# A transformer block in one kernel: the last tiles' norm, logits and hits ahead of other work, square roots moved, the first maxima alone

## The chip, the cores and the metric

The kernel runs on one core of one Trainium2 chip. The metric is the time on the device of one execution, in microseconds; the kernel is run several times and the median is given. A profile is one further execution, recorded by the hardware profiler; its span runs from the first to the last instruction.

Engines by their names in the profile: PE is TensorE (PEld its weight loads), DVE is VectorE, ACT is ScalarE, POOL is GpSimd, and SP, the sync engine, issues most of the DMAs.

## What is computed

A transformer block on x of 8 x 256 x 512 in float32: x = x + attention(layernorm(x)), then x = x + ffn(layernorm(x)). The reference, cut to its core:

```python
qkv = h @ w_qkv                       # 32 query heads, 8 key/value heads, D = 128
scores = einsum('bqhgd,bkhd->bhgqk', q, k) * D ** -0.5
bias = -slopes * sqrt(max(pos_q - pos_k, 0)); -inf where pos_k > pos_q
out = einsum('bhgqk,bkhd->bqhgd', softmax(scores + bias), v) @ w_o

dots = softmax(x @ centroids.T / 0.1)           # 64 clusters
hits = dots > 0.01
query_sel, cluster_sel = any(hits, axis=1), any(hits, axis=0)
row_sel = cluster_sel[assignments]              # one flag for each of 512 columns
dense = x @ weight.T + bias
out = where(query_sel[:, None] & row_sel[None, :], dense, 0)
```

`cluster_sel` asks whether any token of the whole batch hits a cluster, so no output column is settled before the last tile's hits are known.

## The kernel before

The 2048 tokens are 16 tiles of 128 rows (`NT`); four tiles, that is two batch entries, form a pair (`PT_TOK`, `NPAIR` = 4). A unit `u` is one batch entry and one key/value head with its four query heads, so there are 64 units (`NU`), 16 to a pair (`slot` is the unit's place in its pair). One loop runs over the units, and two more passes drain it. Its body is an order written out by hand (`manual_schedule`): each engine executes its instructions in the order in which the program text issues them.

A pass of the loop does in turn the scores of unit u, the softmax of unit u-1, and the value product and output projection of unit u-2:

- `scores(u, 0..2)` (L358) makes keys-by-queries scores in PSUM on PE; DVE scales them and adds the position bias into `s` (L372, L378).
- `over_keys` (L384) takes maxima or sums over the keys on DVE (L387, L388, L390). `over_quadrants` (L392) transposes the result on PE (L397, `tp_r`), finishes it on DVE (L401, L404), writes the row to memory (L406) and reads it back to all partitions (L415), both on SP's queue. Normally one transpose serves the maxima of u and the sums of u-1; a unit for which `alone` holds sends its maxima earlier (`rows_max`). `subtract_max` takes the maxima away, one part on POOL (L422), one on DVE (L425), and ACT takes the exponential (L724, in the last unit L775).
- `attend` (L429) makes the value products (L446, L447) and DVE multiplies by the inverse sums (L450).
- All projections use a seven-product scheme of 2 x 2 blocks. `a_sums` and `b_sums` (L107, L120) make the block sums S1 to S4 and T1 to T4 on POOL (`gp`) or DVE (`ve`). `strassen` (L136) runs step i of a q, k or v projection; `project_out` (L454), called as `w(i)`, that of the output projection. Products 1, 6, 7 and 4 gather in one PSUM bank, and a copy on ACT (L158; L483 into `snap`) must be done before the next of them may be added.
- In some slots a pair of tiles is normalised: `norm_stats` on DVE (L259, L260), `norm_root` on ACT (L267; square root and exponential need different tables, and the load stands as its own instruction), `norm_scale` on DVE (L272, L274), `norm_write` on ACT (L281), and later `transpose_into` on PE (L290) with a copy out of PSUM (L291).
- The feed-forward part of finished pairs goes tile by tile in parts `f(0)` to `f(3)`: `ffn_transpose`, `ffn_logits` with `ffn_exp` and `ffn_dense` (L535), `ffn_bias_add` (L542), and `ffn_hits`, `ffn_qsel`, `ffn_end` (L547 to L562).

In the normal unit the order around the change is:

```python
f(2), norm(0), e(4), e(3), x(0), w(1), x(1), sum_old(), w(5, 6), qq(3), w(2)
rows(), behind_rows(), w(7, 3), norm(2), w(4)
```

where `norm(0)` is statistics and root, `norm(1)`, inside `behind_rows`, the scale and `norm(2)` the write; `e(i)` and `qq(i)` are steps of a k or v and of a q projection.

After the loop come the last four tiles, 12 to 15 (`last` = 12), whose x is complete only then: norms, transposes, logits, exponentials, hits, dense products. Then the row selection: `cnt` counts the hits of each cluster (L862), `csel` is its flag (L864), and `rsel` (L866) spreads it over the 512 columns with the one-hot matrix of the assignments, which `onehot_of_columns` (L580) made in unit 4. At last the output of 16 tiles: three (`SPLIT`) on POOL with a copy `rsel_sb` of the selection (L880 to L882), thirteen on DVE with a predicated copy (L896), stored from the queues of SP and ACT in turn (L897). x and y of the first two pairs were put aside in memory and are read back in unit 63 (L834, four loads of 1 MB).

## Time and profile before

| what | value |
|---|---|
| median of three runs | 1461.13 us (1459.53 to 1461.52) |
| the profiled execution, its own time | 1461.43 us |
| its span | 1459.6 us |
| PE busy | 1412.7 us, 97% of the span |
| DVE busy | 934.0 us, 64% |
| POOL busy | 879.4 us, 60% |
| ACT busy | 369.2 us, 25% |
| granted PE clock, mean | 0.994 of full speed |
| moved by DMA | 189.94 MB, 130 GB/s on average |

In timeline rows the columns are start, length, engine, line, operation, and the tile written, then those read; in brackets stands how long the engine had been idle and what released it. In the rows of stretches each engine has its busy microseconds and its count of instructions, then follow the granted PE clock, the busy share of the DMA engines and GB/s. "SPq" is a DMA issue on SP's queue. Matmuls overlap in the records, so that the length of a row of several is a little more than the time that they take from the engine.

### The profile page before, as it was taken

To read this page: it belongs to the slowest core of one execution; us is meant where nothing else is said; L and a number is where in the kernel's file an instruction comes from. 1 tells how busy PE (TensorE), PEld (TensorE's weight loads), DVE (VectorE), ACT (ScalarE), POOL (GpSimd) and SP (SyncE) were. 2 spreads that over 40 slices of the span, in tenths; PEclk is the share of its full clock that TensorE was granted. 3 is DMA by queue.
4 is the path that set the end of the run, shared out by engine and by line. 5 is a ranking of instruction groups with operands and counts; after the bars stand their busy time and mean duration, and the time that the engine had idled before them with its cause. 6 is when DMAs were issued, how large, how long until landed. Compare 5 with 4: busy or idle time off the path is not lost.

```text
span 1459.6 us, 16530 instructions
## 1 busy us (share of the span) xinstructions
PE 1412.7 (97%) x5859; PEld 1076.0 (74%) x5859; DVE 934.0 (64%) x1708; ACT 369.2 (25%) x648; POOL 879.4 (60%) x885
## 2 busy tenths in 40 slices
PE   8899999999999999999999999999999999999985
PEld 7676777767877678777777677777777777877562
DVE  4467656676566666658655666566756676566766
ACT  3221222421232222331213312142222222122331
POOL 6376867667465654557655466556756675566544
PEclk9999999999999999999999999999999999999998
DMA  5235333443242544424342524424332343243343
GB/s 187 75 132 174 130 95 139 158 145 117 101 159 73 173 140 150 158 83 143 108 147 99 161 86 173 165 110 145 130 114 97 123 174 131 87 159 102 102 145 115
DMA packets 85968, 189.94 MB, mean 130 GB/s; under 512 B 10592, under 2 KB 18784, under 8 KB 85888
## 3 DMA queue, kind: packets, MB, share of 16 engines
q1 hardware_dynamic: 84736, 186.41, 37.2%
q10 hardware_dynamic: 864, 1.57, 0.3%
q8 instruction: 47, 0.77, 0.2%
q0 software_dynamic: 288, 0.92, 0.2%
q14 instruction: 33, 0.27, 0.1%
HBM read 175.77 MB, written 13.11 MB: 129 GB/s over the span
## 4 chain that ended last, share of the span: by engine, by line
PE 86%; DVE 8%; issue 2%; POOL 2%; ACT 1%; DMA 0%; POOLq 0%; DVEq 0%; ACTq 0%
PE ps_oa L468 14%; PE ps_qa L145 13%; PE sc L370 7%; PE ps_oc L468 7%; PE ps_qc L145 7%; PE av L446 6%; PE sc L376 4%; PE ps_ob L468 4%; PE ps_va L145 4%; PE ps_ka L145 4%; PE ps_f L535 4%; PE av L447 3%; PE ps_qb L145 3%; PE ps_vc L145 2%; PE ps_kc L145 2%
## 5 line engine op out<-in xcount | busy, mean ns | idle before, releaser
L500 POOL TENSOR_TENSOR x<-x,snap 128x256 f32<-128x256 f32 x189 | 136.1, 735 | 182.7 <-DVE x L488 110.7
L422 POOL TENSOR_TENSOR s<-s,bc 128x1024 f32<-128x1024 f32 x64 | 151.6, 2368 | 151.7 <-DMA bc<-row_hbm 144.1
L112 POOL TENSOR_TENSOR o_s<-oT 128x256 f32<-128x256 f32 x64 | 47.6, 744 | 191.3 <-DVE oT L450 187.4
L387 DVE TRANSPOSE_TENSOR_REDUCE r<-s 128x32 f32<-128x1024 f32 x128 | 157.9, 1234 | 4.4 <-ACT s L724 4.4
L158 ACT COPY qT<-ps_qa 128x512 f32<-128x512 f32 x128 | 74.7, 583 | 284.5 <-PE ps_qa L145 284.5
L483 ACT COPY snap<-ps_oa 128x256 f32<-128x256 f32 x189 | 70.3, 372 | 278.7 <-PE ps_oa L468 278.7
L468 PE MATMUL ps_oa<-wo,oT 128*128 128x256 f32 x512 | 133.5, 383 | 6.6 <-DVE oT L450 4.2
L724 ACT ACTIVATE s<-s 128x1536 f32<-128x1536 f32 x63 | 93.5, 1484 | 153.1 <-DVE s L425 147.2
L446 PE MATMUL av<-s,v 128*128 128x512 f32 x256 | 131.6, 596 | 0.0
L145 PE MATMUL ps_qa<-xT,wq 128*128 128x256 f32 x512 | 121.1, 380 | 0.8 <-ACT qT L158 0.8
L370 PE MATMUL sc<-qT,kT 128*128 128x512 f32 x256 | 120.3, 592 | 0.0
L145 PEld LDWEIGHTS ps_qa<-xT,wq 128*128 128x128 f32 x512 | 97.1, 190 | 27.6 <-issue 16.0
L468 PEld LDWEIGHTS ps_oa<-wo,oT 128*128 128x128 f32 x512 | 90.6, 190 | 28.6 <-DVE oT L450 8.3
L372 DVE SCALAR_TENSOR_TENSOR s<-sc,alibi 128x512 f32<-128x512 f32 x128 | 88.1, 691 | 29.0 <-PE sc L370 28.1
L378 DVE SCALAR_TENSOR_TENSOR s<-sc,alibi 128x512 f32<-128x512 f32 x64 | 44.3, 692 | 83.7 <-PE sc L376 83.7
L447 PEld LDWEIGHTS av<-s,v 128*128 128x128 f32 x256 | 49.0, 191 | 61.7 <-issue 61.7
L450 DVE TENSOR_TENSOR oT<-av,bc 128x512 f32<-128x512 f32 x128 | 84.1, 683 | 14.2 <-PE av L447 12.3
L388 DVE TRANSPOSE_TENSOR_REDUCE r<-s 128x16 f32<-128x512 f32 x128 | 85.7, 669 | 0.0
L488 DVE TENSOR_TENSOR x<-x,ps_ob 128x256 f32<-128x256 f32 x64 | 27.0, 421 | 79.5 <-PE ps_ob L468 79.4
L447 PE MATMUL av<-s,v 128*128 128x256 f32 x256 | 76.4, 380 | 0.0
L390 DVE TENSOR_TENSOR r<-r 128x16 f32<-128x16 f32 x128 | 72.4, 566 | 4.4
L370 PEld LDWEIGHTS sc<-qT,kT 128*128 128x128 f32 x256 | 48.5, 190 | 33.9 <-issue 29.9
(177 smaller groups left out, 2973.0 us busy)
## 6 DMA issues: line engine op xcount, KB each, us to landing
bc<-row_hbm SPq DMA_DIRECT2D x128, 512.0 KB, 4.9
wq<-in_w_qkv SPq DMA_DIRECT2D x32, 1024.0 KB, 7.7
wo<-in_w_o SPq DMA_DIRECT2D x32, 1024.0 KB, 7.8
alibi<-al_hbm SPq DMA_DIRECT2D x24, 512.0 KB, 8.5
wk<-in_w_qkv SPq DMA_DIRECT2D x16, 512.0 KB, 9.4
wv<-in_w_qkv SPq DMA_DIRECT2D x8, 1024.0 KB, 10.9
x<-in_x SPq DMA_DIRECT2D x16, 256.0 KB, 9.4
al_hbm<-alibi SPq DMA_DIRECT2D x8, 512.0 KB, 9.1
```

The costliest lines, as they stand in the source:

```text
L145: nc.tensor.matmul(bank[:, cols], lhsT=lhsT, rhs=rhs, start=first and j == 0, stop=j == len(mms) - 1, skip_group_check=True)
L370: nc.tensor.matmul(sc, lhsT=kT[:, t0 : t0 + P], rhs=qT[:, hh : hh + 2, t0 : t0 + S], start=True, stop=True)
L372: nc.vector.scalar_tensor_tensor(s[:, hh * S : (hh + 2) * S], sc, D ** -0.5, bias[:, hh : hh + 2, :].rearrange("p h q -> p (h q)"), ALU.mu ...
L387: nc.vector.tensor_reduce(first, s[:, :K0].rearrange("p (j q) -> p j q", q=32), AX.X, op, apply_transpose=True)
L388: nc.vector.tensor_reduce(second, s[:, K0:].rearrange("p (j q) -> p j q", q=32), AX.X, op, apply_transpose=True)
L422: gp(k0, k0, mx, sub)
L446: nc.tensor.matmul(av, lhsT=v[:, i0, vc], rhs=pT[:, hh * S : (hh + 2) * S], start=True, stop=False)
L447: nc.tensor.matmul(av3[:, :, P:S], lhsT=v[:, i0 + 1, vc], rhs=pT[:, K0 + hh * P : K0 + (hh + 2) * P].rearrange("p (h q) -> p h q", h=2), s ...
L450: ve(oT[:, e].rearrange("p k m q -> p k (m q)"), av3, inv[:, hh : hh + 2, :], ALU.mult)
L468: nc.tensor.matmul(bank[:, :HH], lhsT=x[:, e, :], rhs=y[:, e, :], start=first and e == 0, stop=e == 1, skip_group_check=True)
L500: gp(c, c, s, ALU.add)
L724: nc.scalar.activation(s_sb[u - 1], s_sb[u - 1], AF.Exp)
```

## The change

- The norm has four parts now: statistics, root, scale, write. The root goes from behind `f(2)` to behind `w(5, 6)`.
- `onehot_of_columns` goes from ahead of unit 4 to behind its `qq(2)`.
- Unit 0 sends its maxima alone, as the last two units do, and S3 and S4 of the first v weights are made before the loop.
- In the opening, the second pair of tiles gets its scale and write after tile 1 is transposed and copied, and tile 3 is transposed ahead of `k(2)`.
- In pass 64 the value products go ahead of a feed-forward transpose. In pass 65 the hits of tile 11 go ahead of the projection, and tile 13's transpose, tile 14's norm and both logits products of tiles 12 and 13 go into the pass.
- After the loop, maxima, exponentials and hits of the four last tiles go ahead of most dense products; tile 13's product is split in two around the row selection (`ffn_dense` takes `chunks`); the ends of tiles 11 to 13 go ahead of the predicated copies; two products of bias and flag go from POOL to ACT.

```diff
--- before.py
+++ after.py
@@ -509,32 +509,42 @@
     ffn_sb = {}
     SPLIT = (1, 2, 3)
 
-    def ffn_logits(t):
+    def ffn_logits_product(t):
         xnT = xnT_sb[t]
         lg = p_sc.tile([P, 512], F32, tag="sc", name="lg")
         for c in range(NC_H):
             nc.tensor.matmul(lg[:, :NCL], lhsT=xnT[:, c, :], rhs=cent[:, c, :],
                              start=c == 0, stop=c == NC_H - 1)
+        ffn_sb[t] = lg
+
+    def ffn_max(t):
+        lg = ffn_sb[t]
         nmax = small.tile([P, 1], F32, tag="cmax", name="cmax")
         nc.vector.tensor_reduce(nmax, lg[:, :NCL], AX.X, ALU.max, negate=True)
         nc.vector.tensor_scalar(nmax, nmax, 1.0 / TEMPERATURE, None, ALU.mult)
         ffn_sb[t] = lg, nmax
 
-    def ffn_exp(t):
+    def ffn_logits(t):
+        ffn_logits_product(t)
+        ffn_max(t)
+
+    def ffn_exp(t, e=None):
 
         lg, nmax = ffn_sb[t]
-        e = small.tile([P, NCL], F32, tag="e", name="e", bufs=3)
+        if e is None:
+            e = small.tile([P, NCL], F32, tag="e", name="e", bufs=3)
         esum = small.tile([P, 1], F32, tag="esum", name="esum")
         nc.scalar.activation(e, lg[:, :NCL], AF.Exp, bias=nmax, scale=1.0 / TEMPERATURE, accum_out=esum)
         ffn_sb[t] = e, esum
 
-    def ffn_dense(t, w_ffn):
+    def ffn_dense(t, w_ffn, chunks=range(NC_H)):
         xnT = xnT_sb[t]
-        ps = p_acc.tile([P, 512], F32, tag="acc", name="ps_f")
-        for c in range(NC_H):
+        if 0 in chunks:
+            y_sb[t] = p_acc.tile([P, 512], F32, tag="acc", name="ps_f")
+        ps = y_sb[t]
+        for c in chunks:
             nc.tensor.matmul(ps, lhsT=xnT[:, c, :], rhs=w_ffn[:, c, :],
                              start=c == 0, stop=c == NC_H - 1)
-        y_sb[t] = ps
 
     def ffn_bias_add(t, y=None):
         if y is None:
@@ -602,8 +612,9 @@
     found23 = norm_stats(2, 3)
     norm_tile(0, 0)
     sum_x(0, "")
-    normalise(found23, tags=("y", "y"))
+    found23 = norm_root(found23)
     norm_tile(0, 1, tp=tp1, copy=nc.vector.tensor_copy)
+    norm_write(norm_scale(found23), tags=("y", "y"))
     alibi_bias(0)
     sum_weights(gp, wk, (0, 0), D, "S1")
     load_wv(0, 0, wk[0, 0]["S1"])
@@ -616,13 +627,13 @@
     k, q = project_k(0, 0), project_q(0)
     k(1)
     norm_tile(0, 2, tp=tp2, copy=nc.vector.tensor_copy)
+    norm_tile(0, 3)
     k(2)
-    norm_tile(0, 3)
     sum_x(0, "T1 T2 T3 T4")
     a_sums(gp, wq[0], "S3 S4")
-    q(1), q(2), k(6), k(7), k(5), k(4), k(3), q(6), q(7), q(5)
-    sum_weights(ve, wv, (0, 0), HH, "S1 S2")
-    q(4), q(3)
+    q(1), q(2), k(6), k(7), k(5), k(4), k(3)
+    sum_weights(ve, wv, (0, 0), HH)
+    q(6), q(7), q(5), q(4), q(3)
     a_sums(gp, wq[1], "S1 S2 S3")
     w_ffn = None
     y_late = None
@@ -705,14 +716,14 @@
         def norm(part):
             nonlocal found
             if t_norm is not None:
-                found = (lambda _: norm_root(norm_stats(t_norm, t_norm + 1)), norm_scale, norm_write)[part](found)
+                found = (lambda _: norm_stats(t_norm, t_norm + 1), norm_root, norm_scale, norm_write)[part](found)
 
         def max_and_old():
             scores(u, 2)
             over_keys(s_sb[u], r, 0, ALU.max)
             if old:
                 subtract_max(u - 1, 1)
-            if own and slot in (0, 8):
+            if u > 0 and slot in (0, 8):
                 a_sums(ve, wv[p, slot // 8], "S3 S4")
 
         def more_sums():
@@ -727,19 +738,20 @@
             if old:
                 over_keys(s_sb[u - 1], r, 1, ALU.add)
 
-        alone = NU - 2 <= u < NU
+        alone = u == 0 or NU - 2 <= u < NU
 
         def rows_max():
             if alone:
                 over_quadrants(u, r, True, False)
 
         def rows():
-            over_quadrants(u, r, own and not alone, old)
+            if old:
+                over_quadrants(u, r, own and not alone, True)
 
         def behind_rows():
 
             f(3)
-            norm(1)
+            norm(2)
             if own and (slot == 7 or slot == 15 and more_p):
                 sum_weights(ve, wv, (p, 1) if slot == 7 else (p + 1, 0), HH, "S1 S2")
             if more_p and slot == 13:
@@ -755,38 +767,39 @@
             if more_p and slot in (11, 12):
                 norm_tile(p + 1, 2 * (slot - 11) + i)
 
-        if u == 4:
-            onehot_of_columns(asg)
         if bb == 0 and own:
             qq(1), e(1), max_and_old(), e(2), f(0), av(0), e(6), exp_old(), av(1), more_sums(), rows_max(), f(1), e(7), qq(2)
-            f(2), norm(0), e(5), e(4), qq(6), e(3), x(0), w(1), x(1), sum_old(), w(5, 6), qq(7), w(2)
-            rows() if old else over_quadrants(u, r, True, False)
-            behind_rows(), w(7, 3), norm(2), w(4)
+            if u == 4:
+                onehot_of_columns(asg)
+            f(2), norm(0), e(5), e(4), qq(6), e(3), x(0), w(1), x(1), sum_old(), w(5, 6), norm(1), qq(7), w(2)
+            rows(), behind_rows(), w(7, 3), norm(3), w(4)
         elif u < NU - 1:
             e(1), qq(4), e(2), max_and_old(), f(0), e(6), av(0), exp_old(), e(7), av(1), f(1), e(5), qq(5)
-            f(2), norm(0), e(4), e(3), x(0), w(1), x(1), sum_old(), w(5, 6), qq(3), w(2)
-            rows(), behind_rows(), w(7, 3), norm(2), w(4)
+            f(2), norm(0), e(4), e(3), x(0), w(1), x(1), sum_old(), w(5, 6), norm(1), qq(3), w(2)
+            rows(), behind_rows(), w(7, 3), norm(3), w(4)
         elif own:
 
             max_and_old(), f(0), av(0), exp_old(), av(1), rows_max(), f(1)
-            f(2), norm(0), w(1), sum_old(), w(5, 6, 2)
+            f(2), norm(0), w(1), sum_old(), w(5, 6), norm(1), w(2)
             rows(), subtract_max(u, 0), subtract_max(u, 1)
-            f(3), norm(1), w(7)
+            f(3), norm(2), w(7)
             nc.scalar.activation(s_sb[u], s_sb[u], AF.Exp)
-            w(3), norm(2), w(4)
+            w(3), norm(3), w(4)
         elif bb == 0:
-            sum_old(), f(0), av(0), av(1), rows(), f(1), w(1, 5), f(2), w(6, 2, 7, 3, 4), f(3)
+            sum_old(), av(0), av(1), f(0), rows(), f(1), w(1, 5), f(2), w(6, 2, 7, 3, 4), f(3)
         else:
             av(0), f(0), av(1), f(1)
             normalise(norm_stats(last, last + 1), tags=("y", "y"))
+            ffn_hits(t_ffn), ffn_qsel(t_ffn)
             w(1), f(2), w(2, 5, 6)
             ffn_transpose(last)
             w(3)
             found = norm_root(norm_stats(last + 2))
+            ffn_transpose(last + 1, "snap")
             w(7)
-            ffn_logits(last)
+            norm_write(norm_scale(found))
+            ffn_logits_product(last), ffn_logits_product(last + 1)
             w(4)
-            f(3)
 
 
         for dst, src in stores:
@@ -838,24 +851,18 @@
 
 
     y_of = lambda i: y_last[i // 2][:, i % 2, :]
-    norm_write(norm_scale(found))
     ffn_dense(last, w_ffn)
-    ffn_transpose(last + 1, "snap")
     normalise(norm_stats(last + 3))
-    ffn_exp(last)
-    ffn_logits(last + 1)
-    ffn_exp(last + 1)
+    ffn_max(last), ffn_exp(last)
+    ffn_max(last + 1), ffn_exp(last + 1)
     ffn_transpose(last + 2, copy=nc.vector.tensor_copy)
-    ffn_dense(last + 1, w_ffn)
     ffn_transpose(last + 3, "o_s", tp=p_acc.tile([P, 512], F32, tag="acc", name="tpx_late"), copy=nc.vector.tensor_copy)
-    ffn_hits(last), ffn_qsel(last), ffn_bias_add(last, y_of(0))
-    ffn_logits(last + 2)
-    ffn_exp(last + 2)
-    ffn_logits(last + 3)
-    ffn_hits(last + 1)
-    ffn_exp(last + 3)
-    ffn_hits(last + 2), ffn_hits(last + 3)
-    ffn_dense(last + 2, w_ffn)
+    ffn_logits_product(last + 2), ffn_logits_product(last + 3)
+    ffn_max(last + 2), ffn_exp(last + 2)
+    ffn_max(last + 3), ffn_exp(last + 3, work.tile([P, NCL], F32, tag="kT", name="e_last", bufs=2))
+    ffn_dense(last + 1, w_ffn, (0, 1))
+    for i in range(4):
+        ffn_hits(last + i)
 
 
     cnt = p_tp.tile([P, 512], F32, tag="tp", name="cnt")
@@ -864,17 +871,19 @@
     nc.vector.tensor_scalar(csel, cnt[:NCL, :P], 0.0, None, ALU.is_gt)
     rsel = p_tp.tile([P, 512], F32, tag="tp", name="rsel")
     nc.tensor.matmul(rsel, lhsT=csel, rhs=onehot, start=True, stop=True)
-    ffn_dense(last + 3, w_ffn)
-    for i in (2, 3, 1):
+    ffn_dense(last + 1, w_ffn, (2, 3))
+    for i in (2, 3, 0):
         ffn_qsel(last + i)
-    ffn_bias_add(last + 1, y_of(1))
+
+    for i in (2, 3):
+        nc.scalar.activation(y_of(i), bias_bc, AF.Copy, scale=ffn_sb[last + i])
+        gp(y_of(i), y_of(i), x2[last + i], ALU.add)
+    ffn_end(last - 1), ffn_bias_add(last, y_of(0)), ffn_end(last), ffn_qsel(last + 1)
+    ffn_dense(last + 2, w_ffn)
     rsel_sb = work.tile([P, H], F32, tag="s", name="rsel_sb", bufs=3)
     nc.scalar.copy(rsel_sb, rsel)
-
-    for i in (2, 3):
-        gp_y = y_of(i)
-        nc.gpsimd.tensor_scalar(gp_y, bias_bc, ffn_sb[last + i], None, ALU.mult)
-        gp(gp_y, gp_y, x2[last + i], ALU.add)
+    ffn_dense(last + 3, w_ffn)
+    ffn_bias_add(last + 1, y_of(1)), ffn_end(last + 1)
     for t in SPLIT:
         xt, yt = back[0][0][:, t, :], back[0][1][:, t, :]
         gp(yt, yt, rsel_sb, ALU.mult)
@@ -887,8 +896,6 @@
         p, i = divmod(t, TPP)
         if t >= last + 2:
             nc.vector.scalar_tensor_tensor(y_of(i), y_sb[t], ffn_sb[t], y_of(i), ALU.mult, ALU.add)
-        elif t >= last:
-            ffn_end(t)
         if p < NPAIR - 2:
             xt, yt = back[p][0][:, i, :], back[p][1][:, i, :]
         else:
```

## The prediction, made before the changed kernel was run

> **What bounds the kernel now.** I read the page first: how much of the span TensorE is busy, and what the chain that ended last is made of.
>
> ```profile
> span 1459.6 us, 16530 instructions
> PE 1412.7 (97%) x5859; PEld 1076.0 (74%) x5859; DVE 934.0 (64%) x1708; ACT 369.2 (25%) x648; POOL 879.4 (60%) x885
> PE 86%; DVE 8%; issue 2%; POOL 2%; ACT 1%; DMA 0%; POOLq 0%; DVEq 0%; ACTq 0%
> ```
>
> TensorE (PE) is the bound in the loop. The change takes no matmul away, so it can only win in the 46.9 us in which PE is idle (1459.6 - 1412.7). The view of what PE waited for (total, times, longest) says where these lie ahead of the last stretch:
>
> ```profile
> PE ps_oa L468 <- ACT snap L483: 6.1, 10, 1.3
> PE ps_oa L468 <- DVE oT L450: 4.2, 3, 1.6
> PE tpx L290 <- ACT xn L281: 3.6, 1, 3.6
> ...
> PE ps_oa L468 <- ACT kT L158: 2.5, 3, 0.8
> PE ps_va L145 <- DVE wv L116: 2.0, 2, 1.7
> ```
>
> Each has a place in the timeline. A copy of a product out of PSUM is late where ScalarE's queue holds a square root: its table load, then a wait for VectorE's statistics, stand in front of the copy.
>
> ```profile
> 244.53 1.28 ACT L267 ACT_TABLE_LOAD   x1
> ...
> 246.38 0.30 ACT L267 ACTIVATE rstd<-mv,eps 128x2 f32<-128x2 f32 x1 [0.57 <-DVE mv L260]
> ...
> 247.56 1.10 PE L468 MATMUL ps_oa<-wo_t,o_s 128*128 128x256 f32 x4 [0.36 <-ACT snap L483]
> ```
>
> Of the last 18 us PE takes 2.5. The chain in order of time (start, length, what) shows who does the rest:
>
> ```profile
> 1435.48 3.49 PE ps_f L535 x8
> ...
> 1439.70 1.14 PE rsel L866 x2
> ...
> 1445.66 1.29 POOL back_xT L880
> ...
> 1455.99 0.60 POOLq L918
> ```
>
> The dense product stands ahead of the row selection `rsel`; then GpSimd (POOL) writes three tiles while VectorE (DVE) writes thirteen, ending at 1454.62.
>
> **The square roots.** By the instruction order, twelve roots (L267) go behind the copies of out-projection steps 1 and 6, past both snap copies and a q, k or xT copy; the count of table loads does not change. The waits they cause, from the timeline: 0.36, 0.82, 0.18, 0.78, 1.28, 0.82, 0.17, 0.78, 0.17, 0.82 in the loop, 0.89 at 1347 and 1.35 at 1385: 8.4 us, which is the 6.1 and 2.5 of the view less 0.16 at 81 us that no root causes. The new place must hide 1.28 + 0.30 = 1.58 us. At the first one the snap copy of step 6 ends at 249.1, so the root ends at 250.6; the next q copy is due at 250.4 (its bank is wanted in the next unit, 5 us on) and the next snap copy at 252.3. At 273 the slack to the snap is 1.6 us. Cover that goes costs at most 1.58 each. The page "ScalarE: Activation LUTs" of the Trainium skill, section "What ACT_TABLE_LOAD costs", speaks against it: it counts a drain too, about 2.66 us a switch. The trace has none: the load at 1413.26 takes 1.28 and the root starts at 1414.56. With 2.96 for both the root would end at 252.0, still ahead of 252.3, so my sum stands by either; only the 273 kind (three places) would lose about 1.4 each, 4 us in all. Behind a waiting root stand snap 7 and the xn writes; statistics were done 2 to 3 us before. The 1.35 is not won: there DVE ends r (L390) at 1386.63, and PE's tp_r waits for it. That leaves 7.1; I take **6.4**, as some early arrivals will meet a DVE or POOL wait (L450, L112). Bounds 3 and 7.1.
>
> **The one-hot rows.** Six DVE operations stood in front of the third score evacuation of unit 4, one of them 2.46 us beside POOL's L422; PE then waited 1.59 for L450 and 0.17 for o_s. They move behind L450 and the q addition; POOL's iota moves behind the four o_s sums. There DVE waits for the iota until about 122.5 and the key sums end about 125.3, where PE's tp_r comes at about 125.9. **1.6**, bounds 1.0 and 1.8.
>
> **The opening.** (a) The copy of tile 1 goes ahead of reciprocal and shift: the first k product starts at about 9.0 instead of 9.64, but tiles 2 and 3 come 0.4 later and their transposes stand in front of k(2); T1 starts 0.5 earlier. Net 0.3. (b) The S3, S4 sums of wv leave DVE's queue in unit 0, where PE waited 1.7 for them, for 21.5 to about 26.3, when DVE is idle (5.8 us before 27.35) and wv has landed (15.5). In their place tp_r waits for the maxima, which end 0.1 us before L116 did: tp_r at 38.4 and L145 at 38.5 instead of 39.30. Gain 0.8 with (a). (c) The maxima of unit 0 go to memory at about 39 instead of 48.76; on SP's queue the row, its broadcast and behind them wq, alibi and wk all go 9 us earlier. L422 runs at 46, POOL's weight sums at 50 to 59 instead of 59 to 68. So they now lie beside DVE's L390 and L425 in unit 1, and such pairs exclude each other: L425 took 0.68 alone and 1.70 beside POOL. The exponential would start 0.4 earlier, not 0.8, and PE's 1.48 wait for r shrink by 0.6 (L390 there 0.82, free 0.18). Sum **1.2**, bounds -0.5 and 2.8.
>
> **The end.** Four steps.
> In unit 64 the two av products (2.6 us) go ahead of the transpose that waited 3.60 for xn. That wait also halved the clock:
>
> ```profile
> 1393.00:1394.00 1.00, 0.68 (x3) 0.68 (x4) 1.00 (x2) 0.98 (x2) 1.00 (x3) 0.50 0.78 262
> ```
>
> (column PEclk 0.50). PE's tp_r then waits for r (1395.06), so logits start at 1395.3 instead of 1398.12: 2.8 earlier. But the next L450 waits for a broadcast whose row sits behind the 4 MB loads in SP's queue:
>
> ```profile
> SPq L415 <- DMA row_hbm<-row: 6.3, 1, 6.3
> ```
>
> It lands near 1410.1, whatever PE does, against L450 at 1410.79. From there: L450 to 1411.5, maximum 1411.9, statistics 1413.4, exponential and table load 1413.8, root, scale 1414.6, the moved hits 0.87, L481 at 1415.5 (it was 1416.74). Then, each at its trace duration: w(6) about 1416, transposes of tiles 12 and 13, logits of both 1419.7 to 1421.5, w(4), dense(12) 1422.4 to 1425.8, transposes of 14 and 15, exponentials of 12 and 13 behind one 1.28 table load to 1427.4 (both score banks are held until then), logits of 14 and 15 to 1428.9, two exponentials to 1429.9, four hits of 0.63 from 1429.4 to 1431.9, cnt, csel, rsel to **1433.9**. Before it was 1440.8.
> Behind it: DVE does three qsel (0.45), three ends of the L562 kind and two bias additions: alone 0.75 and 0.68 each, 1.7 beside POOL as at 1447.04. Between 3.6 and 5.5 us; I take 4.4, so the thirteen copies start at 1437.5 instead of 1441.48. They take 13 x 0.67 + 2 x 0.74 = 10.2, as no L562 stands between them any more, so DVE ends about 1447.8. ScalarE takes POOL's two bias products (0.8 each, from the xn row) ahead of rsel_sb, which is ready at 1435.1; POOL's additions then end at 1436.3 and its three tiles (10.9) at 1447.2 instead of 1456.6. dense(13) to (15) end at 1442.5, ahead of their readers.
> The stores may bind: 16 tiles are 4.19 MB.
>
> ```profile
> 1444.00:1446.00 2.00, 0.46 (x2) 0.00 (x0) 2.00 (x5) 0.00 (x0) 1.92 (x3) 1.00 1.03 381
> ```
>
> The last column is GB/s: the DMA engines are already full while DVE alone stores a tile each 0.64 us. At 381 GB/s the stores need 11.0 us; the first copy ends about 1438.2, so the last lands about 1450.6 (1.4 us to the first data), against 1450.2 from DVE's end and a landing of 2.4. The page "DMA: Bandwidth & Descriptors", section "Where 436 GB/s comes from", lets HBM bind at about 358 GB/s per core: 11.7 us, an end 0.7 later. The trace shows more on the same stores, so I keep 381. Last landing to the end of the span took 1.2 (1456.0 + 2.4 against 1459.6). New end 1451.8 with nothing else changed: **7.8** won, bounds 4.5 and 9.2 (the lower if hits, transposes or exponentials each wait once more, the higher if DVE's additions run alone).
>
> **Sum.** 6.4 + 1.6 + 1.2 + 7.8 = 17.0. The profiled execution took 1461.43 (1.8 more than its span), so 1444.4; the median of the runs, 1461.13, is 0.3 below that execution, so **1444.1**.
>
> **Rivals.**
> (A) The end is held. If the row's landing keeps L450 at 1410.8, the one chain from there to rsel stretches by a wait or two (DVE's hits stand in front of L481, on which w(6) waits; two score banks serve four tiles), and stores and POOL's additions collide, the end wins 4 instead of 7.8 and the roots 5: 1449.3. For it: handovers between four engines in 25 us. Against: the PE work between is unchanged and each duration is in the trace.
> (B) The opening loses. POOL's sums, 9 us earlier, block L390 and L425 twice, the v copy behind the exponential is 1.5 us later than before instead of 0.4 earlier, and PE's longer idle halves its clock once more, as it did between 62 and 65 us after only 2.2 us (a window at 0.50 cost about 1.7). Opening -2.5 instead of 1.2: 1447.8. For it: L425's 1.70. Against: POOL is done by 59. The same place can go the other way: a shorter wait that does not halve the clock gives 1.7 more, 1442.4.
> (C) Slower: the roots in their new place are late. If the root ends after product 7 wants the copy, each of twelve places pays the 1.58 and, when PE idles over 2 us, a half-clock window of 1.7, 3.3 in all: 39.6 against the 10.6 of the other parts gives 1490; with 1.58 alone, 19.0, it is 1469.5, which I take. It decides from 0.9 us a place. For it: at 273 the slack is 1.6 us, and a root that waits for statistics has waited 4.82 (at 820). Against: those statistics end at 820.6 and the step-6 copy at 823.3.
>
> **How the numbers follow.** My forecast 0.62; (A) 0.17; (B) 0.14; (C) 0.07. Executions before lay within 2 us, so 0.2% (2.9 us) is about what a measurement can tell from no change. The forecast, A and B are all over that; of C's 0.07 I leave 0.02 to a small loss that ends within it: faster 0.93, same 0.02, slower 0.05. Range: the low bounds of all parts together give 1453.1, the high ones 1440.2 and with the clock window 1438.5. I take 1438.5 to 1452.5, which holds the forecast, most of A and B, and not C.
>
> **What would show it.** In the changed profile: PE's waits on snap and kT (L483, L158) behind roots gone but for 0.2 and one at unit 63; at each root the table load stands after a snap copy and PE shows no gap; no 1.59 on L450 near 121 us; the tp_r wait of unit 0 about 1.1 where L116 had 1.7; no half clock at the transpose of unit 64; L450 of unit 65 starting on the broadcast; rsel's end about 41 us after unit 63's exponential ends (1440.8 - 1392.6 = 48 before); POOL's three tiles starting about 15.5 us before the end; DMA rows at 380 GB/s through the last 12 us. I am wrong if rsel moves by less than 4 us against unit 63's exponential, if waits of over 1 us stand at the new roots, or if the stores end later than DVE's last copy plus 4 us.

## The result and the profile after

The changed kernel took 1441.32 us, the median of four runs (1439.02 to 1441.55), beside 1460.33 us of the kernel before: ratio 0.9868 with a 95% interval of 0.9851 to 0.9885, so 19.3 us faster (16.8 to 21.8). In a second comparison (below) the ratio was 0.9891 (0.9875 to 0.9907). The forecast was 1444.1 us; the 17.0 us of its sum lie between the two ratios' 15.9 and 19.3 us. The profiled execution took 1441.13 us, its span 1439.4. Its page, with the chain that ended last:

```profile
span 1439.4 us, 16533 instructions
PE 1407.5 (98%) x5859; PEld 1072.9 (75%) x5859; DVE 928.2 (64%) x1708; ACT 372.2 (26%) x650; POOL 878.2 (61%) x883
PE 90%; DVE 6%; issue 1%; ACT 1%; POOL 1%; DMA 1%; DVEq 0%; POOLq 0%; ACTq 0%; SPq 0%
```

PE executes the same 5859 products, is idle for 31.9 us where it was 46.9, and carries 90% of the last chain where it carried 86%. Its busy time fell too, by 5.2 us. What PE waited for (total, times, longest):

```profile
PE tp_r L397 <- DVE r L390: 5.6, 5, 1.4
PE ps_oa L468 <- DVE oT L450: 2.6, 2, 1.5
...
PE tpx L290 <- ACT xn L281: 2.1, 3, 1.0
...
PE cnt L869 <- DVE hits_any L559: 1.3, 1, 1.3
...
PE ps_oa L468 <- ACT snap L483: 0.4, 1, 0.4
```

The 8.6 us in front of copies out of PSUM (6.1 on snap, 2.5 on kT) are gone but for 0.4 at 78 us, where no root stands; of the wait for oT the 1.59 of unit 4 went too. The 3.6 for xn in unit 64 became 1.0; two shorter waits for xn (0.9 and 0.2) now stand in the opening. The place of a root, in the timeline (the one shown of before at 244 to 248 us):

```profile
243.16 0.37 ACT L483 COPY snap<-ps_oa 128x256 f32<-128x256 f32 x1 [1.30 <-PE ps_oa L468]
243.55 1.28 ACT L267 ACT_TABLE_LOAD   x1
244.85 0.30 ACT L267 ACTIVATE rstd<-mv,eps 128x2 f32<-128x2 f32 x1
```

The table load follows the snap copy of step 6 at once, the root follows the load at once, and PE's next groups have no bracket, that is no wait. The Trainium skill's page "ScalarE: Activation LUTs", section "What ACT_TABLE_LOAD costs", adds a drain of about 1.38 us to the load at each switch of tables. Here copy, load and root follow one another within 0.02 us, so no drain is seen, nor was one in the trace of before.

Where the time came from is read by laying the same instruction of both traces side by side. The exponential of each unit on ACT is such a mark; the table gives how many us earlier it starts than in the profile of before.

| exponential of unit | after | roots alone | one-hot alone | opening alone | end alone |
|---|---|---|---|---|---|
| 1 | 2.8 | 1.7 | -3.2 | 4.0 | 1.5 |
| 2 | 2.8 | 1.7 | -3.2 | 4.0 | 1.5 |
| 4 | 4.9 | 1.6 | -1.0 | 4.0 | -0.2 |
| 8 | 4.9 | 1.6 | -1.0 | 4.0 | -0.2 |
| 28 | 10.5 | 7.2 | -0.7 | 5.0 | -1.2 |
| 48 | 13.1 | 10.0 | -0.8 | 4.9 | -1.2 |
| 63 | 15.4 | 10.7 | 0.3 | 4.5 | -0.4 |
| end of the span | 20.2 | 12.1 | 0.4 | 3.1 | 6.1 |

The last four columns are the experiments that follow. The steps in a column are what counts, and not all of them come from the change. In some executions the granted clock falls to 0.50 for about 3.4 us; such a stretch is called a half-clock window below and costs about 1.6 us. Windows near 10 and 65 us make the -3.2 of the one-hot column, one at 121 us makes the fall from 1.5 to -0.2 in the last column, and one at 309 us lies in both. Other moves of 1 to 2 us, which have no part of the change in them either, were not traced.

### The profile page after: what moved, and what is told of

Same layout as the page of the kernel before. It is cut to its first block, busy times and chain, and to the rows that moved or that the text cites. A ratio compares the mean times of both kernels' runs of the same rounds, so it can differ in the third digit from the quotient of the medians.

```text
span 1439.4 us, 16533 instructions
## 1 busy us (share of the span) xinstructions
PE 1407.5 (98%) x5859; PEld 1072.9 (75%) x5859; DVE 928.2 (64%) x1708; ACT 372.2 (26%) x650; POOL 878.2 (61%) x883
## 4 chain that ended last, share of the span: by engine, by line
PE 90%; DVE 6%; issue 1%; ACT 1%; POOL 1%; DMA 1%; DVEq 0%; POOLq 0%; ACTq 0%; SPq 0%
PE ps_qa L145 14%; PE ps_oa L468 14%; PE ps_oc L468 7%; PE sc L370 7%; PE ps_qc L145 7%; PE av L446 7%; PE sc L376 4%; PE ps_ob L468 4%; PE ps_ka L145 4%; PE ps_va L145 4%; PE av L447 3%; PE ps_qb L145 3%; PE ps_f L546 3%; PE ps_kc L145 2%; PE ps_vc L145 2%
## 5 line engine op out<-in xcount | busy, mean ns | idle before, releaser
L450 DVE TENSOR_TENSOR oT<-av,bc 128x512 f32<-128x512 f32 x128 | 83.9, 683 | 11.8 <-PE av L447 10.5
L494 DVE TENSOR_TENSOR x<-x,ps_oc 128x256 f32<-128x256 f32 x128 | 53.3, 416 | 30.5 <-PE ps_oc L468 29.6
```

The costliest lines, as they stand in the source:

```text
L450: ve(oT[:, e].rearrange("p k m q -> p k (m q)"), av3, inv[:, hh : hh + 2, :], ALU.mult)
```

## The experiments

**One part at a time, in the kernel before.** Four kernels, timed together on one chip against 51 runs of before.

The roots:

```diff
-  found = (lambda _: norm_root(norm_stats(t_norm, t_norm + 1)), norm_scale, norm_write)[part](found)
+  found = (lambda _: norm_stats(t_norm, t_norm + 1), norm_root, norm_scale, norm_write)[part](found)
...
-  w(5, 6), qq(7), w(2)
+  w(5, 6), norm(1), qq(7), w(2)
...
-  rows(), behind_rows(), w(7, 3), norm(2), w(4)
+  rows(), behind_rows(), w(7, 3), norm(3), w(4)
...
```

> The kernel before with one part of the change alone: the square root of each layer norm is taken after the seventh step of the output product, apart from the statistics. The prediction's term for it is 6.4 us, the listed waits of TensorE on these roots less what stays. Theory, from the shifts between the two traces: each wait costs its listed time and about 0.24 us more in the first group behind it, ten places, so about 10 us; a time near 1450.3 us. Rival: the listed waits are all of it, and the rest of the 15.4 us by unit 63 came from elsewhere; a time near 1453.9 us. In both, no wait of a projection's first group on an exponential in the two units of a norm.

Measured: 1449.81 us, ratio 0.9937 (0.992 to 0.9953), that is 9.2 us (6.9 to 11.7). The table says the same: from unit 8 to unit 63 its exponentials gain 9.1 us. The interval alone would also allow the 7.1 us of listed waits, so the places decide. One of them, by PE's groups in the kernel before:

```profile
820.01 1.03 PE L468 MATMUL ps_oc<-wo_t,o_s 128*128 128x256 f32 x4
821.82 1.10 PE L468 MATMUL ps_oa<-wo_t,o_s 128*128 128x256 f32 x4 [0.78 <-ACT snap L483]
822.75 1.89 PE L145 MATMUL ps_qa<-xT,wq 128*128 128x256 f32 x8
```

and with the roots moved:

```profile
812.39 1.03 PE L468 MATMUL ps_oc<-wo_t,o_s 128*128 128x256 f32 x4
813.25 1.03 PE L468 MATMUL ps_oa<-wo_t,o_s 128*128 128x256 f32 x4
814.12 1.89 PE L145 MATMUL ps_qa<-xT,wq 128*128 128x256 f32 x8
```

From ps_oc to ps_qa is 2.74 us before and 1.73 here: 1.01 gained, where the bracket says 0.78. Products of a flowing pipe overlap (a row of 1.03 starts 0.86 behind the last one); behind a wait 0.17 of that overlap is missing, and the next group starts 0.06 later than it otherwise does. Measured in this way, each of the eleven places takes 0.22 to 0.26 us more than its bracket lists: 9.7 us together for 7.1 listed.

The one-hot rows:

```diff
-  if u == 4:
-      onehot_of_columns(asg)
...
   qq(1), e(1), max_and_old(), e(2), f(0), av(0), e(6), exp_old(), av(1), more_sums(), rows_max(), f(1), e(7), qq(2)
+  if u == 4:
+      onehot_of_columns(asg)
```

> The kernel before with the one-hot matrix of the columns alone moved, behind unit 4's first half. The prediction's term is 1.6 us; the shift of the traces between units 3 and 6 says about 2.2 us. A time of 1458.1 to 1458.7 us if either holds. Rival: the work on VectorE that is moved delays something later in unit 4, and the two traces' shift had another cause; then within 0.5 us of before.

Measured: 1457.46 us, ratio 0.9991 (0.9982 to 1.0001): 1.3 us, with an interval from nothing to 2.6. The time alone can't tell this from no change; the table can, since from unit 2 to unit 4 this kernel and the changed one both gain 2.15 us. PE in the kernel before:

```profile
118.42 1.89 PE L145 MATMUL ps_qa<-xT_t,wq_s 128*128 128x256 f32 x8
121.89 1.30 PE L468 MATMUL ps_oa<-wo,oT 128*128 128x256 f32 x4 [1.59 <-DVE oT L450]
123.31 1.13 PE L468 MATMUL ps_oc<-wo_t,o_s 128*128 128x256 f32 x4
```

and with the rows moved:

```profile
121.61 1.89 PE L145 MATMUL ps_qa<-xT_t,wq_s 128*128 128x256 f32 x8
123.34 1.03 PE L468 MATMUL ps_oa<-wo,oT 128*128 128x256 f32 x4
124.20 1.03 PE L468 MATMUL ps_oc<-wo_t,o_s 128*128 128x256 f32 x4
```

From ps_qa to ps_oc it is 4.89 before and 2.59 here. That is 2.3 for listed waits of 1.76, and some 0.2 is given back at the unit's tp_r, which comes 1.06 behind the group ahead of it and not 0.87.

The opening:

```diff
-  normalise(found23, tags=("y", "y"))
+  found23 = norm_root(found23)
   norm_tile(0, 1, tp=tp1, copy=nc.vector.tensor_copy)
+  norm_write(norm_scale(found23), tags=("y", "y"))
...
+  norm_tile(0, 3)
   k(2)
-  norm_tile(0, 3)
...
-  q(1), q(2), k(6), k(7), k(5), k(4), k(3), q(6), q(7), q(5)
-  sum_weights(ve, wv, (0, 0), HH, "S1 S2")
-  q(4), q(3)
+  q(1), q(2), k(6), k(7), k(5), k(4), k(3)
+  sum_weights(ve, wv, (0, 0), HH)
+  q(6), q(7), q(5), q(4), q(3)
...
-  alone = NU - 2 <= u < NU
+  alone = u == 0 or NU - 2 <= u < NU
...
```

> The kernel before with the opening alone changed: unit 0's maxima go through TensorE by themselves and early, the second half of the first value weights' sums comes earlier, the last tile is transposed before the third step of k, and the second pair's root stands apart from its scale. The prediction's term is 1.2 us. Theory: about 2.8 us, of which about 1.7 is a window of half clock in unit 1 (62 to 65 us) that no longer falls, so a time near 1457.5 us with the granted clock at 1.00 through 60 to 66 us. Rival: the window of half clock is not the opening's doing and stays; then 1459.1 us, with 0.50 in the slices from 62 to 65 us.

Measured: 1457.99 us, ratio 0.9983 (0.9975 to 0.9991): 2.5 us (1.3 to 3.7). Its exponentials are 4.0 us ahead by unit 1, but in the kernels with the roots or the end alone, whose opening is that of before, they are 1.7 and 1.5 ahead. The stretches from 60 us on say why (columns as in the table of the profile before). The kernel before, then the one with the end alone, then the one with the opening:

```profile
62.00:64.00 2.00, 2.00 (x6) 1.55 (x6) 0.67 (x2) 0.22 (x1) 2.00 (x3) 0.50 0.00 0
```

```profile
62.00:64.00 2.00, 2.00 (x11) 1.76 (x10) 0.97 (x3) 0.37 (x1) 2.00 (x2) 1.00 0.00 0
```

```profile
62.00:64.00 2.00, 1.66 (x8) 1.13 (x6) 2.00 (x3) 0.00 (x0) 0.00 (x0) 1.00 0.00 0
```

Before, PE executed six products in two microseconds at a granted clock of 0.50; with the same opening and no window it executed eleven at 1.00. Between 61 and 68 us a window fell in two of the four profiles with the old opening (before and the one-hot kernel) and in none of the nine with the new one. It is worth about 1.6 us when it falls; whether the new opening keeps it away, thirteen profiles do not show. The nine profiles with the new opening have unit 1's exponential 2.2 to 4.0 us ahead of before, 2.9 on average. Less 1.6, the opening itself gains 0.6 to 2.4 us, 1.3 on average (1.2 in the changed kernel's profile, 2.4 in this kernel's).

The end: unit 64's order, and with it all that the diff shows of unit 65 and of what follows the loop, including the split of `ffn_logits` and `ffn_dense`.

```diff
-  sum_old(), f(0), av(0), av(1), rows(), f(1), w(1, 5), f(2), w(6, 2, 7, 3, 4), f(3)
+  sum_old(), av(0), av(1), f(0), rows(), f(1), w(1, 5), f(2), w(6, 2, 7, 3, 4), f(3)
...
```

> The kernel before with the end alone changed: unit 64's order, and all that follows unit 65's first product (logits of two tiles together, first threshold hits, the dense product of tile 13 in two halves, bias times row on ScalarE, ends ahead of the copies). The prediction's term is 7.8 us, a time near 1452.5 us. Theory, from the two traces: 4.8 us (1455.5 us), because unit 64 loses 1.7 us to a half clock after its waits, and because the stores then leave back to back at about 376 GB/s from the first copy to the end, 4.19 MB in 11.2 us. Rival: the end is worth its 7.8 us by itself and lost it only behind the other parts; then 1452.5 us.

Measured: 1454.86 us, ratio 0.9963 (0.9953 to 0.9973): 5.4 us (3.9 to 6.9), against the 7.8 of the forecast. The four ratios add to 18.4 us, the whole change had 15.9 and 19.3. So the runs show no part that helps or hinders another; with each ratio uncertain by 1.2 to 2.5 us they could not show a small one.

To see where the end's 7.8 shrank, three lengths are taken from each profile: from the end of unit 63's exponential to the end of `rsel`, from there to the last copy's end, and from there to the span's.

| kernel | half clock in unit 64 | exponential to rsel | rsel to last copy | last copy to end |
|---|---|---|---|---|
| before | yes | 48.3 | 13.8 | 5.0 |
| before with the roots moved | no | 46.8 | 13.8 | 5.0 |
| before with the one-hot rows moved | yes | 48.1 | 13.8 | 5.0 |
| before with the opening changed | yes, two | 49.6 | 13.8 | 5.0 |
| before with the end changed | no | 41.5 | 14.1 | 5.0 |
| after | yes | 43.1 | 14.1 | 5.1 |
| after, second profile | yes | 43.1 | 14.1 | 5.0 |

The row selection moved as forecast (41.3) where the clock held. A window of half clock in unit 64 costs about 1.5 of it, before and after alike. The equal 5.0 in the last column has two causes: before, POOL's third tile ended last; after, the stores do. Behind the selection nothing was won: 19.1 us where the forecast had 17.9 and the kernel before 18.8. The changed kernel's chain in order of time:

```profile
1419.14 1.12 PE rsel L873 x2
1420.26 1.93 PE ps_f L546 x4
...
1422.21 0.70 DVE y_kT L552
...
1424.68 0.73 DVE back_xT L903
...
1433.61 0.72 DVE x L903
```

DVE has the three ends of tiles 11 to 13 in front of the copies. The timeline gives their whole lengths:

```profile
1419.39 0.73 DVE L572 SCALAR_TENSOR_TENSOR y_late<-y_late,qsel,x 128x512 f32<-128x512 f32 x1
1420.76 1.10 DVE L572 SCALAR_TENSOR_TENSOR y_kT<-y_kT,qsel,x 128x512 f32<-128x512 f32 x1
1422.94 1.82 DVE L572 SCALAR_TENSOR_TENSOR y_kT<-y_kT,qsel,x 128x512 f32<-128x512 f32 x1
```

The copies start 4.4 us behind the selection: tile 13's bias and end wait for the second half of its dense product, and the two ends beside POOL take 1.10 and 1.82 us where the first, ahead of POOL's work, takes 0.73. And the stores no longer keep up:

```profile
1428.00:1430.00 2.00, 1.04 (x3) 0.19 (x1) 2.00 (x4) 0.00 (x0) 1.62 (x3) 1.00 1.01 374
1430.00:1432.00 2.00, 0.00 (x0) 0.00 (x0) 2.00 (x4) 0.00 (x0) 1.90 (x3) 0.85 1.03 375
1432.00:1434.00 2.00, 0.00 (x0) 0.00 (x0) 1.93 (x4) 0.00 (x0) 1.60 (x2) 0.50 1.04 381
1434.00:1436.00 2.00, 0.00 (x0) 0.00 (x0) 0.34 (x1) 0.00 (x0) 0.00 (x0) 0.50 1.03 374
```

The DMA engines are full from the first store to 1437.6, at 374 to 381 GB/s, so 16 tiles take 11.2 us from wherever the first one starts. The Trainium skill's page "DMA: Bandwidth & Descriptors", section "Where 436 GB/s comes from", has HBM bind at about 358 GB/s, which is half of what it gives for the two cores of a stack. This kernel runs on one core, and its stores stay above that figure.

**Is it the stores?** In the changed kernel seven copies go ahead of the ends of tiles 11 to 13:

```diff
...
-  ffn_end(last - 1), ffn_bias_add(last, y_of(0)), ffn_end(last), ffn_qsel(last + 1)
+  ffn_bias_add(last, y_of(0))
...
-  ffn_bias_add(last + 1, y_of(1)), ffn_end(last + 1)
...
   for t in range(NT):
+      if t == last - 2:
+          ffn_qsel(last), ffn_end(last - 1), ffn_end(last), ffn_qsel(last + 1)
+          ffn_bias_add(last + 1, y_of(1)), ffn_end(last + 1)
```

> The changed kernel with the order on VectorE after the row selection alone altered: the first seven predicated copies (tiles 0 and 4 to 9) go ahead of the ends of tiles 11, 12 and 13, with their stores; nothing is added or left out. Theory: in the changed kernel the stores run back to back at 375 to 381 GB/s from the first copy to the end, so they set it. With first stores about 4 us earlier the queue is no longer behind, and the end is the last copy (unchanged) and one store's landing, 3.5 us: about 1.9 us less than the changed kernel, 1439.4 us. Rival: the last copy sets the end with a fixed 5.1 us behind it; then no gain (1441.3 us), though the stores are spread over a longer stretch.

Measured: 1443.81 us, ratio 0.988 (0.9863 to 0.9897), not below the changed kernel. Half of the theory held: in its profile the last copy is only 3.3 us ahead of the end, not 5.1, as the queue has run empty. But DVE's part grew from 14.1 to 16.8 us:

```profile
1427.97 2.40 DVE L572 SCALAR_TENSOR_TENSOR y_late<-y_late,qsel,x 128x512 f32<-128x512 f32 x1
1430.29 1.75 DVE L572 SCALAR_TENSOR_TENSOR y_kT<-y_kT,qsel,x 128x512 f32<-128x512 f32 x1
...
1432.80 1.42 DVE L572 SCALAR_TENSOR_TENSOR y_kT<-y_kT,qsel,x 128x512 f32<-128x512 f32 x1
```

Moved behind the copies, the three ends fall beside POOL's work on its three tiles and take 5.6 us, where they took 3.65 in the changed kernel; a copy or a product that reads PSUM takes 0.64 to 0.73 there all the same. From the row selection to the end it takes 20.1 us, 1.0 more than in the changed kernel. So the stores held the end, but DVE's ends come right behind them. From this the next idea: the ends must become shorter, not move.

**The half clock of unit 64.** PE waits twice there, just ahead of the window:

```profile
1377.89 0.66 PE L290 MATMUL tpx<-ident,xn 128*128 128x128 f32 x4 [1.02 <-ACT xn L281]
...
1379.77 0.27 PE L397 MATMUL tp_r<-ident,r 128*64 128x128 f32 x1 [1.23 <-DVE r L390]
```

Nine idle products fill these waits:

```diff
   sum_old(), av(0), av(1)
+  pad = p_sc.tile([P, 512], F32, tag="sc", name="pad")
+  for _ in range(4):
+      nc.tensor.matmul(pad[:, :P], lhsT=ones, rhs=ones, start=True, stop=True)
   f(0)
+  for _ in range(5):
+      nc.tensor.matmul(pad[:, :P], lhsT=ones, rhs=ones, start=True, stop=True)
   rows(), f(1), w(1, 5), f(2), w(6, 2, 7, 3, 4), f(3)
```

> The changed kernel with nine idle products of ones with ones (about 0.21 us each, into a bank that nobody reads) put into the two waits of TensorE in unit 64, of 1.02 and 1.23 us; nothing else is changed. Theory: the half clock of unit 64's logits and dense product (1379.9 to 1386 us) follows these waits, so it goes, and 1.7 us with it: 1439.6 us, and 1.00 granted clock through the unit. Rival: the half clock comes from the lower load before them and not from these waits; then the slices stay at 0.50, and the time is that of the changed kernel or a few tenths more.

The unit in the changed kernel's profile, and then with the idle products:

```profile
1380.00:1382.00 2.00, 2.00 (x10) 1.64 (x9) 1.83 (x6) 0.00 (x1) 1.92 (x3) 0.55 1.05 405
1382.00:1384.00 2.00, 2.00 (x4) 0.86 (x3) 0.00 (x0) 0.40 (x2) 1.79 (x3) 0.60 1.05 383
```

```profile
1380.00:1382.00 2.00, 1.88 (x19) 1.72 (x17) 1.97 (x4) 0.46 (x1) 1.92 (x2) 1.00 1.01 391
1382.00:1384.00 2.00, 2.00 (x7) 0.98 (x6) 1.07 (x5) 0.41 (x2) 1.92 (x4) 1.00 1.05 401
```

In this profile the clock holds, and from the exponential to `rsel` it takes 41.5 us, 1.7 less than after. But the time was 1441.01 us, ratio 0.9865 (0.9845 to 0.9885): no gain that is measured.

Over all 13 profiles such windows, about 3.4 us at 0.50, stood at a few places only (the last 15 us, where PE has nothing to do, left out): near 10, 62, 121, 309 and 1170 us, between 1376 and 1397, and near 1420. Each fell in some profiles and not in others with the same code up to there. In unit 64 one fell in three of the four profiles with the old order, and, on the logits and dense product, in three of the five with the new order and no idle products. With the idle products one fell in none of two. Two profiles are too few to say that the products prevent it, and why a window falls or not could not be seen. The windows fit most of the spread between runs: in the 51 runs of before the mean time falls from 1462.1 us at a mean clock of 0.993 to 1458.5 at 0.995.

**The two waits filled by useful work.**

```diff
-  f(2), norm(0), w(1), sum_old(), w(5, 6), norm(1), w(2)
-  rows(), subtract_max(u, 0), subtract_max(u, 1)
-  f(3), norm(2), w(7)
+  f(2), norm(0), w(1), sum_old(), w(5, 6), norm(1)
+  nc.scalar.activation(small.tile([P, 1], F32, tag="warm", name="warm_exp", bufs=1), eps, AF.Exp)
+  w(2)
+  rows(), norm(2), norm(3), subtract_max(u, 0), subtract_max(u, 1)
+  f(3), w(7)
   nc.scalar.activation(s_sb[u], s_sb[u], AF.Exp)
-  w(3), norm(3), w(4)
+  w(3), w(4)
...
-  sum_old(), av(0), av(1), f(0), rows(), f(1), w(1, 5), f(2), w(6, 2, 7, 3, 4), f(3)
+  sum_old(), f(0), av(0), av(1)
+  ffn_logits_product(t_ffn), ffn_dense(t_ffn, w_ffn, (0, 1))
+  rows()
+  ffn_max(t_ffn), ffn_exp(t_ffn), ffn_dense(t_ffn, w_ffn, (2, 3))
+  w(1, 5), f(2), w(6, 2, 7, 3, 4), f(3)
```

> The changed kernel with the two waits of unit 64 filled by work that has to be done anyway: unit 63's norm is scaled and written ahead of the subtraction of the maxima, so that tile 9's transpose doesn't wait, tile 9's logits and half of its dense product go ahead of the transpose of the sums, and one activation of a single column loads the exponential's table right behind the root (1.28 us off the path to unit 63's exponential). Theory: the waits' 2.2 us and the half clock's 1.7 us go, less about 0.5 us that stays: about 3 us, 1438.3 us. Rival: the broadcast of unit 64 lands behind the loads of the first eight tiles' rows (the write before it took 9.1 us to land) and holds unit 65's first VectorE product, so that the wait comes back there; then within 0.5 us of the changed kernel.

Measured: 1441.65 us, ratio 0.987 (0.9856 to 0.9885). No gain, and for neither reason given. The waits of unit 64 are gone, but a new one stands in unit 63:

```profile
1375.11 1.52 ACT L281 ACTIVATE xn<-x,shift,rstd 128x512 f32<-128x512 f32 x2 [1.34 <-DVE shift L274]
1376.53 0.35 ACT L483 COPY snap<-ps_oa 128x256 f32<-128x256 f32 x1
...
1376.93 1.13 PE L468 MATMUL ps_oa<-wo_t,oT 128*128 128x256 f32 x4 [2.18 <-ACT snap L483]
```

The xn writes wait for the shift on DVE and hold the snap copy behind them: the fault that the change had taken away, made again in another place.

**Three things together.** The last edit, the early copies, and this:

```diff
...
+  ffn_hits(last), ffn_hits(last + 1)
   ffn_logits_product(last + 2), ffn_logits_product(last + 3)
...
-  for i in range(4):
-      ffn_hits(last + i)
+  ffn_hits(last + 2), ffn_hits(last + 3)
```

> The changed kernel with three things together: the order of unit 63 and 64 that fills the waits, the threshold hits of tiles 12 and 13 ahead of the logits of 14 and 15 (they end 1.2 us before the count then, and TensorE waited 1.32 us for them), and the predicated copies of seven tiles ahead of the ends of 11 to 13. If each is worth its own estimate (3.0, 1.2 and 1.9 us): 1435.2 us, 1.7% below before. Rival: the parts share one bound, VectorE's 15 us from the row selection to the last copy or the stores' 11.2 us, and only half is left: about 1438.3 us.

Measured: 1439.63 us, ratio 0.9851 (0.9833 to 0.987). The interval overlaps that of the changed kernel. In the trace only the hits show a gain: from the start of unit 64's first output product to the start of `rsel` it takes 32.1 us, in the changed kernel 33.3, and PE's wait of 1.32 us for the hits is gone. The early copies show a loss, as by themselves: 20.1 us from `rsel` to the end. PE's wait for the snap copy in unit 63 stands here too (2.19), and a window fell right behind it, where the last kernel's profile, with the same wait, had none.

**A better end.** From these: hits of tiles 12 and 13 early; their bias product on ACT and sum with x on POOL ahead of the selection, as 14 and 15 have it, so that DVE's end is one operation out of PSUM; tile 11's end in DVE's idle 2.2 us of unit 65; two tiles on POOL, not three.

```diff
-  SPLIT = (1, 2, 3)
+  SPLIT = (1, 2)
...
+  ffn_end(last - 1)
...
+  ffn_hits(last), ffn_hits(last + 1), ffn_qsel(last)
...
+  def bias_and_x(i):
+      nc.scalar.activation(y_of(i), bias_bc, AF.Copy, scale=ffn_sb[last + i])
+      gp(y_of(i), y_of(i), x2[last + i], ALU.add)
+  def end(i):
+      nc.vector.scalar_tensor_tensor(y_of(i), y_sb[last + i], ffn_sb[last + i], y_of(i), ALU.mult, ALU.add)
...
+  bias_and_x(0)
+  ffn_hits(last + 2), ffn_hits(last + 3), ffn_qsel(last + 1)
+  bias_and_x(1)
...
-  ffn_end(last - 1), ffn_bias_add(last, y_of(0)), ffn_end(last), ffn_qsel(last + 1)
+  ffn_qsel(last + 2), ffn_qsel(last + 3)
+  end(0)
...
-  ffn_bias_add(last + 1, y_of(1)), ffn_end(last + 1)
...
```

It ran beside the changed kernel, and once more with the nine idle products:

> The changed kernel itself once more, on the chip and beside the runs of the next two, so that they are compared with it and not with another day's time: 1441.3 us, ratio 0.9868 to before.

> The changed kernel with its last 25 us rearranged: the hits of tiles 12 and 13 go ahead of the logits of 14 and 15 (the run of three together showed the row selection 1.17 us earlier by it), tiles 12 and 13 get bias times row on ScalarE and the sum with x on GpSimd as 14 and 15 do, before the selection is known, so that VectorE's ends (1.10 and 1.82 us beside GpSimd in the changed kernel) become one product and sum out of PSUM of 0.7 us each; tile 11's end goes into VectorE's idle 2.2 us in unit 65; and GpSimd takes two tiles (1, 2) of the last selection, not three. Theory: what sets the end is VectorE's 14.1 us from the row selection to the last copy and the queued stores' 5.1 us behind it; the first copy comes 0.8 us behind the selection, the last some 11.5 us, and the stores' 11.2 us run beside the copies: 15.3 us where the changed kernel takes 19.1, and 1.2 us from the hits: 1436.3 us. Rival: GpSimd becomes the bound through the two sums added to it (1.3 to 1.5 us each) and by slowing down VectorE: then no more than the hits' 1.2 us, 1440.1 us.

> The same as the kernel with the rearranged tail, with the nine idle products in unit 64's waits as well. In two of three profiles without them a window of half clock fell on unit 64's logits and dense product and cost 1.7 us, in one it did not, and with them it did not. Theory: 1.1 us on the mean over runs, 1435.2 us. Rival: the windows fall elsewhere instead, as the medians of the run with the products alone say (1441.0 beside 1441.3 us): the time of the rearranged tail within 0.5 us.

Measured on that chip: the changed kernel 1444.44 us (0.9891, 0.9875 to 0.9907), the new end 1436.44 us (0.9842, 0.9822 to 0.9862), with idle products 1437.94 us (0.9843, 0.9825 to 0.9862). The new end is faster than both kernels beside it: 1.58% below before, and by the two ratios 0.5% below the changed kernel (7.2 us, give or take 3.7). From `rsel` to the span's end it takes 15.4 us; the estimate was 15.3, the changed kernel has 19.1.

```profile
1418.77 1.37 DVE L910 COPY_PREDICATED back_xT<-rsel,back_xT 128x512 f32<-128x512 int32 x2 [0.92 <-ACT rsel_sb L890]
...
1425.56 0.75 DVE L872 SCALAR_TENSOR_TENSOR y_kT<-ps_f,qsel,y_kT 128x512 f32<-128x512 f32 x1
...
1429.48 0.72 DVE L910 COPY_PREDICATED x<-rsel,y_alibi 128x512 f32<-128x512 int32 x1
```

The first copy comes 0.7 us behind the selection, no end takes over 0.75, and the last copy is done 12.1 us behind the selection.

That is 3.7 us. The 1.2 us of the hits did not come: from unit 64's first output product to `rsel` it takes 33.4 us, as in the changed kernel. POOL's new sum of bias and x lies on DVE's last hits:

```profile
1414.72 1.26 POOL L869 TENSOR_TENSOR y_kT<-y_kT,x 128x512 f32<-128x512 f32 x1 [16.31 <-ACT y_kT L868]
1414.81 1.25 DVE L559 TENSOR_TENSOR hits_any<-hits_any,e_last 128x64 f32<-128x64 f32 x1
```

The hits' operation takes 0.23 us elsewhere. Here it ends 0.08 us behind POOL's sum, and PE waits 1.29 us ahead of the count, as in the changed kernel (1.32); the kernel with the idle products shows the same. So the rival named for this run, that POOL slows DVE, is true of the hits. The other 3.5 of the 7.2 us stand in no trace of the end: in the profiles a window at 1168 us and one in unit 64 fell in the changed kernel and not in the new one. That 1436.44 us lies so near to the expected 1436.3 is luck, since the changed kernel itself took 3 us more in this comparison than in the first. The idle products add nothing, as their rival had it.

## Why the prediction was right

- **The bound.** PE's idle time was the main thing to win, and 15.0 of its 46.9 us went. "Only" was wrong: of the span's 20.2 us the other 5.2 came out of PE's busy time. A group behind a wait is longer in the records (1.10 for 1.03 us), and in a half-clock window the lost time counts as busy.
- **Roots, 6.4.** Right in mechanism, too small: 9.2 by its own run, 9.1 by its trace, above the upper bound of 7.1. The sum counted what the view of waits lists and took some off. It left out that each wait also breaks PE's overlap, 0.24 us a place at eleven places. The roots' new place hides them, and none of the waits that rival (C) needed appeared. Nor did a DVE or POOL wait of any size take the roots' place (the largest rise is 0.4, on wv), so almost nothing had to be taken off. The 1.35 at 1385 was rightly left out: there PE's tp_r now waits 1.41 for r.
- **One-hot, 1.6.** Too small by the same term, and above its upper bound of 1.8: 2.15 by the traces. Its own run (1.3, from nothing to 2.6) can't tell.
- **Opening, 1.2.** About right once the clock is set aside: 1.3 on average over nine profiles, 0.6 to 2.4. Its own run gave 2.5 (1.3 to 3.7), with the half-clock window that falls in some executions of before, which rival (B) named as the way up. The tp_r of unit 0 waits 1.01 us where 1.1 was forecast. The way down of (B) did not come: in unit 1 DVE's L390 took 0.18 and L425 0.69, as without POOL.
- **End, 7.8.** Too large: 5.4 by its own run, 4.8 in the changed kernel's profile. The chain to `rsel` was right to 0.2 us where the clock held (41.5 for 41.3). Two terms failed. First, the 48.3 us of before, from which it was subtracted, held a clock window of 1.5 that often falls after the change as well; and the sign "no half clock at the transpose of unit 64" was wrong, since a window fell right behind it. Second, the stretch behind `rsel`: the copies started 4.4 us later, not 3.6, and the last copy was 5.1 us ahead of the end, not 4.0. The queue of stores ran empty 3.3 us behind it (2.8 forecast), and from there to the end it took 1.8 (1.2 forecast). Against that the copies took 9.7, not 10.2. Rival (A) was right in the size of the end (4) and in that stores and sums collide. Its other cause did not hold the end: L450 of unit 65 does start on the broadcast in the kernel with the end alone, as forecast (DVE waits 1.78 us for it), but PE has no wait on it.
- **The sum.** 17.0 forecast; 9.2, 1.3, 2.5 and 5.4 by the four runs. The roots' term was too small and the end's too large, and they cancel: that the total is better than its parts is luck. The forecast also took 0.2% (2.9 us) for what a measurement can tell, from three executions that lay within 2 us; the 51 executions of the later comparison spread over 8.6 us.

## What to carry to other kernels

Price a stall of TensorE by the distance between the starts of the groups around it, compared with the same groups elsewhere, not by the wait that the view lists; and an instruction that waits in an in-order queue is priced by the copies behind it. Ahead of a bound taken from one profile, look at whether a half-clock window lies in it: the difference to a second profile of the same code shows how much of a gain may be luck. At the end of a kernel, work out when the first store can start and what the stores need from there; that end is only met if the engine that feeds them has nothing slow between its copies.

## What the runs showed that was not expected

- Short waits cost more than their listed length: 0.78 us listed is 1.01 us lost, and over eleven places 7.1 us listed are 9.7 lost.
- Windows of half clock fall at a handful of places and only in some executions of the same code: behind waits of 1.0 and 1.2 us in unit 64 in three profiles of five. With nine idle products in these waits none fell there in two profiles, but the median did not move.
- DVE's product and sum of operands in SBUF took 1.1 to 2.4 us beside POOL and 0.75 alone, and even its hits of 64 columns took 1.25 instead of 0.23. Its predicated copies with the selection in PSUM took 0.64 us beside POOL.
